# A two-layer block on one core: three places where the written order of TensorE's work is changed

## The chip, the core and the metric

The kernel runs on one core of a Trainium2 chip. A core has five engines with a queue each: TensorE (PE in the profile; its weight loads are listed as PEld), VectorE (DVE), ScalarE (ACT), GpSimd (POOL) and SyncE (SP), which here issues most of the DMA transfers. The metric is the device time of one execution in microseconds (us).

## The reference

Everything is float32. `x` and `ctx_1024` are 8 sequences (B) of 256 tokens (S) of 256 features (D), 2048 tokens (T) in all. Four residual steps follow each other:

```python
x = x + L0_xattn(layernorm(x), ctx, ctx)   # 1
x = x + L0_ffn(layernorm(x))               # 2
x = x + L1_xattn(layernorm(x), ctx)        # 3
x = x + L1_ffn(layernorm(x))               # 4
```

1. Sequences are projected to 16 features (`Wq`) after they are regrouped as 4 of 512 rows. The cyclic correlation of query and key over the features, averaged over everything else, gives a few weights and shifts. The value is rolled by each shift, summed with the weights, repeated for 16 heads and multiplied with `Wout`.
2. Eight experts with exactly 256 tokens each. Expert 0 takes the 256 tokens with the highest score against its centroid, expert 1 the best 256 of those left, and so on:

```python
for e in range(E):
    s = where(taken, -inf, scores[:, e]); _, idx = top_k(s, C); taken[idx] = True
h = gelu(einsum('ecd,edf->ecf', layernorm(routed), w1) + b1)   # F = 1024
out = routed + einsum('ecf,efd->ecd', h, w2) + b2              # back in token order
```

3. Cross attention with 16 heads of 16 features. Each sequence attends to the 256 rows of its own context, then comes an output product with `Wp`.
4. A mixture of experts: a router (softmax, top 2 of 8 experts), experts with `silu(x w1) * (x w3)` and `w2` of 1024 hidden features, and a shared expert of the same size; half of each is added.

## The kernel before, in words

The work is in one function, `fast_path`; `general_path` is there for data that do not fit the fast one's assumptions; every line that the trace names lies in the fast one. The tokens lie in SBUF as 16 tiles of 128 tokens on the partitions (P = 128), two tiles to a sequence (TPB = 2), in the tensor X. From line 1271 on the order is written by hand: each engine executes its instructions in the order in which the source calls them, and no scheduler moves them. If an instruction must wait for another engine, everything behind it on its own engine's queue waits too. Four stages follow each other in the trace.

**Front, 0 to 62 us.** Transposes of x and the context, scores' raw products and the correlation. Its last part is touched by the change. `copy_rows` (L1851) multiplies the two tiles of a sequence with the identity into a PSUM bank (`po`), without closing the sum; five of these are issued in a row, for the sequences `order_b[0]` to `order_b[4]`. Then come the "small products": `pb` (L1886, 8x8, which spreads the bound of each expert's scores over the partitions) and three pairs into `pw` (L1889, 32 columns each), which lie in one bank (tag "pg" of the pool `ps_a`, which has a single buffer). VectorE copies them out (`WCn`, `bound`). The same buffer is then used for `pr3` (L1924, four products of 128 columns: value times rolled weights), which VectorE scales to `R3` (L1932), and for `pp` (L1935, two products of 256 columns with `Wout`), to which VectorE adds the bias, giving `PB` (L1937). `spread_rows` (L1862, seen at L1867) adds `PB`'s rows to the open sums `po`, so that a bank then holds x after step 1. `take` (L1975) computes the statistics of a bank on VectorE, ScalarE copies it back to X, and its bank is free for the copy of a further sequence. 512 columns of these copies are one record in the trace where the matrix is 128x512.

**Search and expert products of step 2, 62 to 222 us.** For each expert, `search` (L2176) finds the 256th highest score in five rounds (ROUNDS). In a round VectorE counts the tokens above 32 thresholds (`count`), TensorE adds the counts up over the partitions (`pcn`), VectorE narrows the interval (`few`, `k`, `t`) and counts again. `list_tokens` (L2233) turns the chosen tokens into a list of indices in steps: VectorE marks them (`sel`, `taken`, L2245 to L2248), TensorE sums (`pse`, L2253), VectorE scans, TensorE places (`ppl`), VectorE makes two one-hot tensors (`oab`, `ob`, L2288 to L2291), TensorE joins them (`pid`, L2295) and spreads the result (`pix`), and GpSimd gathers the tokens' rows from DRAM (`R`) by an indirect DMA. While expert e is searched, the steps of the list of expert e - 1 are called one per round by `steps_of` (L2458), and `start_ffn` then queues the products of a finished list.

TensorE's idle time in these rounds is filled: `work` is a queue of pieces with a stated cost, and `fill(us)` (L1181) issues pieces until the stated costs reach the argument:

```python
while work and us > 0.3:
    cost, do = work.popleft(); do(); us -= cost
```

One product of an expert (`ph` of L2395 or `py` of L2412, 128x256) is stated at 0.43 us. A round is in the source `fill(each if r else head)`, the `pcn` product, `few`, `t`, the new count, and `next(steps)` at its end. The arguments of `head` and `each` come from FILLS (L2469) for experts 0 to 3 and are 2.58 and 2.58 for the others. The pieces thus stand ahead of `pcn`, and nothing stands between `pcn` and the list's product that `next(steps)` issues. SyncE's queue carries the loads of weights (`load_l0`, L1830), of `wp`, `bvc` and `bpb` before expert 5, and the writes of a blank row to the DRAM table Td (in `ffn`, L2349), which the last stage uses.

**Attention, 222 to about 363 us.** A unit is a sequence b and a half c of its heads. `queries` (L2635) multiplies the transposed normalised tokens `hT` with `wq` into a bank, from which ScalarE writes one half of QM and VectorE the other (L2654). `scores` (L2666) makes four products of 512 columns into `p`, ScalarE takes the exponentials; `values` (L2683) multiplies them with VA (value rows, made by `vals`). Ahead of it, step 2's output is added to X by `add_y` (L2572), which also has SyncE load the y of two sequences later; `batch_stats` (L2577) computes mean and variance on VectorE, a power on GpSimd, and a Newton step on GpSimd or VectorE; `norm_q` (L2611) writes the normalised tokens `h2` with one engine for each of the two tiles (seen at L2602); `turn_q` (L2631) transposes them on TensorE (L2626) and copies them to `hT` on VectorE. `add_bias` (L2615) adds `bpb` to X on GpSimd; `bpb` itself is the bias plus `pbp`, a product that holds one bank of `ps_m` until VectorE has read it. The loop at L2977 issues for each unit the first half of its scores, the values of the unit before, the second half and so on, with these steps between them. In the first units: `turn_q(1)`, `add_y(2)` and `batch_stats(2)` lie in unit (0,0), `norm_q(2)` in the middle of (0,1) with one tile on VectorE and one on GpSimd, `queries(1)` in the last part of (0,0) and `turn_q(2)` at the end of (0,1). `router_weights` (L2794: six small VectorE steps and two transposes of the router's matrix, each copied out by VectorE) is issued at the end of unit (2,0); what needs it is `route`, first called in unit (4,0).

**Step 4, 363 to 891.8 us.** The products of the shared expert and the eight experts; the change touches nothing in it.

Of the kernel before, what the change touches and what calls it, by code (L numbers as in the profile page):

```python
# [9 lines left out]
F32 = mybir.dt.float32  # L10
# [1076 lines left out]
def fast_path(  # L1087
# [785 lines left out]
                skip_group_check=True,  # L1873
            )

    for b in order_b[:4]:
        copy_rows(b, ps_t, "pt")
    copy_rows(order_b[4], ps_k, "pm")
    bnd = pa.tile([E, 1], F32, name="bnd")
    nc.vector.tensor_scalar(bnd, cs[:, 1:2], 1.01, None, ALU.mult)  # L1880
    bdiag = pa.tile([E, E], F32, name="bdiag")
# [1 line left out]
    WCn = pa.tile([P, 3, 32], F32, name="WCn")  # L1883
    pw = ps_a.tile([P, 4, 32], F32, tag="pg", name="pw")
    pb = pw[:, 3, 0:E]
    nc.tensor.matmul(pb, ones[:E, :], bdiag, start=True, stop=True)  # L1886
    for j in range(3):
        for dc in range(KC):
            nc.tensor.matmul(  # L1889
                pw[:, j, :],  # L1890
                wrt[:, dc, j * P : (j + 1) * P] if j < 2 else bt[:, dc, :],
                cenP[:, dc, :],
                start=(dc == 0),
                stop=(dc == KC - 1),
            )
    nc.vector.tensor_copy(WCn, pw[:, 0:3, :])
    bound = pr.tile([P, E], F32, name="bound")
    nc.vector.tensor_copy(bound, pb)
# [19 lines left out]
        allow_small_or_imprecise_dtypes=True,  # L1918
    )

    pr3 = ps_a.tile([P, 2, P], F32, tag="pg", name="pr3")
    for j in range(2):
        for sc in range(2):
            nc.tensor.matmul(  # L1924
                pr3[:, j, :],
                CW[:, sc, j * P : (j + 1) * P],
                vT[:, sc, :],
                start=(sc == 0),
                stop=(sc == 1),
            )  # L1930
    R3 = pa.tile([P, 2, P], F32, name="R3")
    nc.vector.tensor_scalar(R3, pr3, rtot, None, ALU.mult)  # L1932
    pp = ps_a.tile([P, D], F32, tag="pg", name="pp")
    for j in range(2):
        nc.tensor.matmul(pp, R3[:, j, :], woutr[:, j, :], start=(j == 0), stop=(j == 1))  # L1935
    PB = pa.tile([P, D], F32, name="PB")
    nc.vector.tensor_tensor(PB, pp, boutb, ALU.add)  # L1937

# [237 lines left out]
    def search(e, row, steps, head, each):  # L2176
# [25 lines left out]
        if e >= 2:  # L2202
            next(listers[e - 1])
        for r in range(ROUNDS):
            fill(each if r else head)
            pcn = ps_r.tile([P, 32], F32, tag="pcn", name="pcn")
            nc.tensor.matmul(
                pcn, cnt.to_broadcast([P, P]), B32h, start=True, stop=True
            )
            few = pm.tile([P, 32], F32, tag="few", name="few")  # L2210
            k = pm.tile([P, 1], F32, tag="k", name="k")
            nc.vector.tensor_scalar(
                few, pcn, CAP * (e + 1) + 0.5, None, ALU.is_lt, ALU.add, accum_out=k
            )
            if r < ROUNDS - 1:
                t = pm.tile([P, 1], F32, tag="t", name="t")
                nc.vector.scalar_tensor_tensor(
                    t, k, step[:, r, e : e + 1], w, ALU.mult, ALU.add
                )
                cnt = count(t)  # L2220
            nlo = pm.tile([P, 1], F32, tag="lo", name="lo", bufs=4)
            nc.vector.scalar_tensor_tensor(
                nlo, k, step[:, r, e : e + 1], lo, ALU.mult, ALU.add
            )
            lo = nlo
            if r < ROUNDS - 2:
                w = next_low(lo, r + 1)
            if r < ROUNDS - 1:
                next(steps)
        low.append((n, lo))  # L2230
        listers[e] = list_tokens(e, hand_over)
# [234 lines left out]
                start_ffn()  # L2466
            yield

    FILLS = ((0.43, 1.29), (2.15, 1.29), (2.15, 1.73), (2.15, 1.73))  # L2469
    for e in range(E - 1):  # L2470
        if e == 5:

# [8 lines left out]
                    )  # L2481
            nc.sync.dma_start(out=bpb, in_=L1_xattn_bp.partition_broadcast(P))
        search(
            e, rows.get(e), steps_of(e), *(FILLS[e] if e < len(FILLS) else (2.58, 2.58))
        )
        if e == 0:
            for k, _ in enumerate(listers[0]):
# [473 lines left out]
    for i in range(0, 4, 2):  # L2961
        list(vals(i, 2, ps_m))
    norm_q(0, nc.vector, nc.vector)
    nc.vector.tensor_tensor(bpb, bpb, pbp, ALU.add)
    hTs[0] = pq2.tile([P, KC, S], F32, tag="hT", name="hT")
    transpose_tokens(h2s[0], hTs[0], ps_m, "pm", 0)
    add_y(1)
    batch_stats(1, "q", nc.vector)
    queries(0, 0)
    queries(0, 1)  # L2970
    norm_q(1, nc.vector, nc.vector)
    add_bias(0)
    add_bias(1)
# [5 lines left out]
    for b in range(B):  # L2979
        for c in range(NB):  # L2980
            scores(b, c, 0)
            if prev:
                values(*prev, 0)
            send()
# [1 line left out]
                next(gates, None)  # L2986
            if prev is None:
                list(vals(4, 1, ps_m, nc.vector.tensor_copy))
                turn_q(1)
                add_y(2)  # L2990
                batch_stats(2, "q")
            elif c == 0:
                if b >= 2:
                    project_out(b - 2)
            else:
                if b >= 1:
                    turn_back(b - 1)
                if b >= 2:
                    turn_m(b - 2)
                if b + 2 < B:  # L3000
                    norm_q(b + 2, nc.vector, nc.gpsimd)
                    add_bias(b + 2)
            scores(b, c, 1)
            if gates:
# [8 lines left out]
            if gates:  # L3013
                next(gates, None)
            if c == 0:
                if b + 1 < B:
                    queries(b + 1, 0)
                    queries(b + 1, 1)
                if b + 2 < B and b:
# [5 lines left out]
            else:  # L3025
                if b >= 1:
                    turn_out(b - 1)
                if b + 2 < B:
                    turn_q(b + 2)
            if prev is None:  # L3030
# [27 lines left out]
                WS = load_l1(wsp, -1)  # L3058
            if (b, c) == (1, 0):
                router_columns()  # L3060
            if (b, c) == (2, 0):
                router_weights()
            prev = b, c


# [404 lines left out]
```

## Time and profile before

Three runs took 892.38, 890.15 and 886.46 us, with a median of 890.15 us. The profiled execution took 893.59 us by the same measure; its span, from the first to the last record, is 891.8 us, at a mean granted TensorE clock of 0.989 of full speed. The busy times by stage, in us (windows of the trace):

| stage | length | PE | DVE | ACT | POOL | clock | DMA share |
|---|---|---|---|---|---|---|---|
| front, 0-62 | 62 | 56.03 | 35.47 | 21.27 | 26.16 | 0.89 | 0.65 |
| search, 62-136 | 74 | 68.08 | 58.40 | 36.72 | 18.52 | 1.00 | 0.47 |
| search, 136-168 | 32 | 30.43 | 18.11 | 11.58 | 7.12 | 1.00 | 1.08 |
| rest of step 2, 168-222 | 54 | 52.75 | 12.57 | 17.44 | 11.46 | 1.00 | 0.38 |
| attention's start, 222-265 | 43 | 38.38 | 22.20 | 23.88 | 12.97 | 0.96 | 0.39 |
| attention, 265-363 | 98 | 95.41 | 61.20 | 67.03 | 51.01 | 1.00 | 0.05 |
| step 4, 363-891 | 528 | 523.04 | 101.28 | 87.36 | 86.41 | 1.00 | 0.38 |

How to read it: a busy row of the page gives the busy share in 40 slices of the span, 22.3 us each, in tenths; the row PEclk gives the clock that TensorE was granted, in tenths of full speed. In the timeline a line begins with the start in us, then the duration of the group, the engine, the source line, the operation with output and inputs, the shape and the number of instructions; in brackets stands how long the engine was idle before it and which instruction released it. "PE pid L2295 <- DVE ob L2291" in the list of waits means that TensorE's product pid stood for VectorE's ob. Ends of matmuls are modelled, so a busy TensorE may hold small holes.

### The profile page before, as it was taken

The numbers are of one execution on the slowest core, as the hardware profiler recorded it, in microseconds if no ns is written. First come the engines' busy times: TensorE is split into PE (matmuls) and PEld (weight loads), VectorE is DVE, ScalarE is ACT, GpSimd is POOL, SyncE is SP. The second block draws the span as 40 slices with busy tenths as digits, with TensorE's granted clock in tenths as the row PEclk, the third lists the DMA queues.
The fourth block names the chain that finished last, engine by engine and source line by source line (L and its number), as shares of the span: only waits on it lengthen the run. The fifth ranks groups of instructions, "written<-read, shape, count | busy, mean of one in ns | idle before, by whom it ended". The sixth has DMA issues, their size and how long they took to land.

```text
span 891.8 us, 11183 instructions
## 1 busy us (share of the span) xinstructions
PE 864.1 (97%) x4200; PEld 539.3 (60%) x4200; DVE 309.2 (35%) x1026; ACT 265.3 (30%) x495; POOL 213.6 (24%) x294
## 2 busy tenths in 40 slices
PE   9899899999899999999999999999999999999997
PEld 7546677878545555544748574646565656574745
DVE  7368876330635676453111111111111111111021
ACT  3244454242476767431010111111111111111110
POOL 7051221221324655233320011111101132111200
PEclk9879999999999999999999999999999999999999
DMA  7555259850250000081210636464656543311130
GB/s 246 180 175 182 83 174 319 249 189 31 57 151 13 14 7 32 19 324 50 73 55 24 189 107 177 148 182 149 162 170 147 182 92 107 89 12 12 18 101 28
DMA packets 86282, 105.21 MB, mean 118 GB/s; under 512 B 7979, under 2 KB 76812, under 8 KB 86188
## 3 DMA queue, kind: packets, MB, share of 16 engines
q1 hardware_dynamic: 77706, 91.10, 32.0%
q0 software_dynamic: 7920, 13.02, 7.0%
q8 instruction: 35, 0.57, 0.3%
q10 hardware_dynamic: 594, 0.30, 0.1%
q14 instruction: 27, 0.22, 0.1%
HBM read 80.60 MB, written 25.37 MB: 119 GB/s over the span
## 4 chain that ended last, share of the span: by engine, by line
PE 85%; DMA 5%; DVE 5%; POOL 1%; SPq 1%; issue 1%; ACT 1%; ACTq 0%; DVEq 0%; POOLq 0%
PE pgt L3090 19%; PE py L3112 19%; PE pu L3090 18%; PE ph L2395 4%; PE py L2412 4%; PE p L2673 4%; PE pv L2688 3%; DMA Td<-blank 2%; PE pp L2739 2%; PE pp L2640 2%; PE pp L1427 1%; PE po L1853 1%; DMA row<-SCd 1%; PE pgu L3285 1%; PE pt L3146 1%
## 5 line engine op out<-in xcount | busy, mean ns | idle before, releaser
L3099 DVE TENSOR_TENSOR A<-A,pu 128x512 f32<-128x512 f32 x96 | 66.1, 688 | 365.0 <-PE pu L3090 358.4
L3098 ACT ACTIVATE A<-pgt 128x512 f32<-128x512 f32 x96 | 57.4, 598 | 270.9 <-PE pgt L3090 270.8
L3159 POOL DMA_INDIRECT Od<-Y,ids x32 | 49.5, 1546 | 306.7 <-ACT Y L3172 211.6
L3090 PE MATMUL pgt<-RT,wa 128*128 128x512 f32 x256 | 121.1, 595 | 0.0
L3090 PE MATMUL pu<-RT,wb 128*128 128x512 f32 x256 | 120.3, 592 | 0.0
L3112 PE MATMUL py<-wc,A 128*128 128x256 f32 x512 | 111.8, 379 | 0.0
L3112 PEld LDWEIGHTS py<-wc,A 128*128 128x128 f32 x512 | 96.7, 190 | 13.3 <-issue 0.5
L2681 ACT ACTIVATE ex<-p,scale 128x512 f32<-128x512 f32 x128 | 77.2, 691 | 34.1 <-PE p L2673 34.1
L3090 PEld LDWEIGHTS pu<-RT,wb 128*128 128x128 f32 x256 | 48.6, 190 | 61.2 <-issue 60.0
L3090 PEld LDWEIGHTS pgt<-RT,wa 128*128 128x128 f32 x256 | 47.6, 190 | 54.9 <-issue 54.5
L2395 PE MATMUL ph<-RT,w 128*128 128x256 f32 x256 | 61.6, 387 | 2.1 <-ACT A L2404 2.1
L2412 PE MATMUL py<-w,A 128*128 128x256 f32 x256 | 59.7, 385 | 0.0
L2395 PEld LDWEIGHTS ph<-RT,w 128*128 128x128 f32 x256 | 45.4, 189 | 10.3 <-ACT A L2404 4.0
L2412 PEld LDWEIGHTS py<-w,A 128*128 128x128 f32 x256 | 47.3, 190 | 6.5
L2404 ACT ACTIVATE A<-ph,b1c 128x256 f32<-128x256 f32 x64 | 30.0, 473 | 69.0 <-PE ph L2395 67.3
L2673 PE MATMUL p<-QM,KT 32*128 32x512 f32 x256 | 45.2, 655 | 2.9 <-DVE QM L2654 2.9
L2913 POOL DMA_INDIRECT Td<-HP,to x32 | 31.6, 987 | 62.2 <-DMA Td<-HP,to 59.3
L3090 PE MATMUL pgt<-HT,wa_-1_2777 128*128 128x512 f32 x96 | 45.5, 596 | 0.0
L3090 PE MATMUL pu<-HT,wb_-1_2778 128*128 128x512 f32 x96 | 45.1, 592 | 0.0
L3172 ACT ACTIVATE Y<-py,R 128x256 f32<-128x256 f32 x32 | 15.2, 474 | 97.0 <-PE py L3112 93.5
L3112 PE MATMUL py<-wc_-1_2779,A 128*128 128x256 f32 x192 | 41.9, 379 | 0.0
L3112 PEld LDWEIGHTS py<-wc_-1_2779,A 128*128 128x128 f32 x192 | 36.4, 190 | 5.8 <-issue 1.0
(463 smaller groups left out, 1001.8 us busy)
## 6 DMA issues: line engine op xcount, KB each, us to landing
w<-in_L_ffn_w_dram SPq DMA_DIRECT2D x16, 1024.0 KB
wa<-in_L_ffn_w_e_dram SPq DMA_DIRECT2D x8, 1024.0 KB
wb<-in_L_ffn_w_e_dram SPq DMA_DIRECT2D x8, 1024.0 KB
wc<-in_L_ffn_w_e_dram SPq DMA_DIRECT2D x8, 1024.0 KB
R<-Td SPq DMA_DIRECT2D x8, 530.0 KB
sa<-in_L_ffn_w_e_dram SPq DMA_DIRECT2D x16, 256.0 KB
sb<-in_L_ffn_w_e_dram SPq DMA_DIRECT2D x16, 256.0 KB
sc<-in_L_ffn_w_e_dram SPq DMA_DIRECT2D x16, 256.0 KB
```

The costliest lines, as they stand in the source:

```text
L2395: nc.tensor.matmul(ph, w1[:, kc, f * P : (f + 1) * P], RT[:, kc, :], start=(kc == 0), stop=(kc == KC - 1),)
L2404: nc.scalar.activation(A[:, f, :], ph, AF.Gelu_apprx_tanh, bias=b1c[:, e, f : f + 1])
L2412: nc.tensor.matmul(py, A[:, f, r * P : (r + 1) * P], w2[:, f, :], start=(f == 0), stop=(f == NF - 1),)
L2673: nc.tensor.matmul(ps[g].rearrange("p m q -> p (m q)"), KT[rows, c, k0 : k0 + P], QM[b][rows, c].rearrange("p m q -> p (m q)"), start=True ...
L2681: nc.scalar.activation(e4[:, g], ps[g], AF.Exp, scale=scale)
L2688: nc.tensor.matmul(pvs[b, c][32 * g : 32 * g + 32, m, :], VA[:, b * TPB + kt, 8 * c + 2 * g + m, :], ex[b, c, kt][:, g, m, :], start=(kt = ...
L2913: nc.gpsimd.indirect_dma_start(out=Td, out_offset=bass.IndirectOffsetOnAxis(ap=to[g][:, k, j : j + 1], axis=0), in_=HP[:, GT * g + j, :], ...
L3090: nc.tensor.matmul(ps, w_[:, kc, fs], xs[kc], start=(kc == 0), stop=(kc == KC - 1),)
L3098: nc.scalar.activation(a, pgt, AF.Silu)
L3099: nc.vector.tensor_tensor(a, a, pu, ALU.mult)
L3112: nc.tensor.matmul(py, A[:, f, s : s + P], wc[:, f, :], start=(f == 0), stop=(f == NF - 1))
L3159: nc.gpsimd.indirect_dma_start(out=Od, out_offset=bass.IndirectOffsetOnAxis(ap=ids, axis=0), in_=Y, in_offset=None, compute_op=ALU.add,)
```

## The change

It edits three places.

*Front.* The copies of `order_b[3]` and `order_b[4]` are issued after the first and the second pair of small products, not before all of them, and `pb` is issued last. A helper `stay_warm` issues a product of the 128x128 matrix of ones with 256 columns of G, of which nothing reads the result: one after the `pr3` group and one after the `pp` group, into the second half of buffers that are made twice as large.

*Search.* From round 1 on 0.86 us less is filled ahead of `pcn`, and 0.86 us is filled after the new count, ahead of the list's step. The amount is now given for each round; that of round 2 of experts 2 and 3 is 2.58 where it was 1.73.

*Attention.* The addition of `pbp` to `bpb` follows the transposes of sequence 0. `queries(0)` comes ahead of `add_y(1)` and `batch_stats(1)`. `turn_q(1)`, `queries(1)`, `add_y(2)` and `batch_stats(2)` move to the middle of unit (0,1). `norm_q(2)`, with both tiles on VectorE, and `add_bias(2)` move to the end of (0,1), directly ahead of `turn_q(2)`. `norm_q(3)`, in unit (1,1), has both tiles on VectorE. `router_weights` moves from the end of unit (2,0) to behind the first half of the scores of unit (3,0).

```diff
-    for b in order_b[:4]:
+    for b in order_b[:3]:
         copy_rows(b, ps_t, "pt")
-    copy_rows(order_b[4], ps_k, "pm")
...
     pb = pw[:, 3, 0:E]
-    nc.tensor.matmul(pb, ones[:E, :], bdiag, start=True, stop=True)
     for j in range(3):
...
+        if j == 0:
+            copy_rows(order_b[3], ps_t, "pt")
+        elif j == 1:
+            copy_rows(order_b[4], ps_k, "pm")
+    nc.tensor.matmul(pb, ones[:E, :], bdiag, start=True, stop=True)
...
-    pr3 = ps_a.tile([P, 2, P], F32, tag="pg", name="pr3")
+    pr3 = ps_a.tile([P, 4, P], F32, tag="pg", name="pr3")
+
+    def stay_warm(ps, n):
+        for _ in range(n):
+            nc.tensor.matmul(ps, ones, G[:, 0, :], start=True, stop=True)
...
+    stay_warm(pr3[:, 2:4, :].rearrange("p a q -> p (a q)"), 1)
     R3 = pa.tile([P, 2, P], F32, name="R3")
-    nc.vector.tensor_scalar(R3, pr3, rtot, None, ALU.mult)
-    pp = ps_a.tile([P, D], F32, tag="pg", name="pp")
+    nc.vector.tensor_scalar(R3, pr3[:, 0:2, :], rtot, None, ALU.mult)
+    pp2 = ps_a.tile([P, 2, D], F32, tag="pg", name="pp")
+    pp = pp2[:, 0, :]
     for j in range(2):
         nc.tensor.matmul(pp, R3[:, j, :], woutr[:, j, :], start=(j == 0), stop=(j == 1))
+    stay_warm(pp2[:, 1, :], 1)
...
         for r in range(ROUNDS):
-            fill(each if r else head)
+            fill(each[r - 1] - 0.86 if r else head)
...
             if r < ROUNDS - 1:
+                fill(0.86)
                 next(steps)
...
-    FILLS = ((0.43, 1.29), (2.15, 1.29), (2.15, 1.73), (2.15, 1.73))
+    FILLS = {0: (0.43, [1.29] * 4), 1: (2.15, [1.29] * 4)}
+    FILLS[2] = FILLS[3] = (2.15, [1.73, 2.58, 1.73, 1.73])
...
-            e, rows.get(e), steps_of(e), *(FILLS[e] if e < len(FILLS) else (2.58, 2.58))
+            e, rows.get(e), steps_of(e), *FILLS.get(e, (2.58, [2.58] * 4))
...
     norm_q(0, nc.vector, nc.vector)
-    nc.vector.tensor_tensor(bpb, bpb, pbp, ALU.add)
     hTs[0] = pq2.tile([P, KC, S], F32, tag="hT", name="hT")
     transpose_tokens(h2s[0], hTs[0], ps_m, "pm", 0)
+    nc.vector.tensor_tensor(bpb, bpb, pbp, ALU.add)
+    queries(0, 0)
+    queries(0, 1)
     add_y(1)
     batch_stats(1, "q", nc.vector)
-    queries(0, 0)
-    queries(0, 1)
...
             scores(b, c, 0)
+            if (b, c) == (3, 0):
+                router_weights()
...
                 list(vals(4, 1, ps_m, nc.vector.tensor_copy))
+            elif b == 0:
                 turn_q(1)
+                queries(1, 0)
+                queries(1, 1)
                 add_y(2)
                 batch_stats(2, "q")
...
-                if b + 2 < B:
-                    norm_q(b + 2, nc.vector, nc.gpsimd)
+                if 2 < b + 2 < B:
+                    norm_q(b + 2, nc.vector, nc.vector if b < 2 else nc.gpsimd)
                     add_bias(b + 2)
...
-                if b + 1 < B:
+                if 0 < b and b + 1 < B:
                     queries(b + 1, 0)
...
                 if b >= 1:
                     turn_out(b - 1)
+                else:
+                    norm_q(2, nc.vector, nc.vector)
+                    add_bias(2)
                 if b + 2 < B:
                     turn_q(b + 2)
...
-            if (b, c) == (2, 0):
-                router_weights()
```

## The prediction

> **What bounds the kernel now.** I read the page's busy rows first. TensorE is busy in 97% of the span and carries 85% of the chain that ended last, so time can only come from its clock or from holes in its queue. The clock row shows two dips.
>
> ```profile
> PE   9899899999899999999999999999999999999997
> PEclk9879999999999999999999999999999999999999
> ```
>
> Windows of half a microsecond (columns: PE, PEld, DVE, ACT, POOL busy, then clock, DMA share, GB/s) date the dips.
>
> ```profile
> 40.00:40.50 0.50, 0.50 (x4) 0.50 (x4) 0.34 (x2) 0.00 (x0) 0.00 (x0) 0.52 0.93 334
> ...
> 53.50:54.00 0.50, 0.50 (x2) 0.00 (x0) 0.08 (x1) 0.50 (x2) 0.24 (x2) 0.83 0.17 63
> ```
> ```profile
> 234.50:235.00 0.50, 0.29 (x4) 0.29 (x8) 0.50 (x2) 0.00 (x0) 0.00 (x0) 0.58 0.00 0
> ...
> 237.50:238.00 0.50, 0.50 (x3) 0.41 (x2) 0.00 (x0) 0.50 (x3) 0.00 (x0) 0.51 0.00 0
> ```
>
> A mean of 0.52 is half clock from 40.02 on; 0.83 is half clock up to 53.67. That is 13.65 us. Likewise 234.58 to 237.99: 3.41 us, a quarter of it. The timeline shows what stood there.
>
> ```profile
> 37.12 0.38 PE L1886 MATMUL pw<-bdiag,ones 8*128 8x8 f32 x2
> ...
> 37.44 1.08 PE L1889 MATMUL pw<-cenP,wrt 128*128 128x32 f32 x8
> ...
> 39.43 1.51 PE L1924 MATMUL pr<-vT,CW 128*128 128x128 f32 x8 [0.47 <-PE pw L1889]
> ...
> 40.98 0.48 DVE L1932 TENSOR_SCALAR R<-pr,rtot 128x256 f32<-128x256 f32 x1 [0.60 <-PE pr L1924]
> ...
> 41.52 2.08 PE L1935 MATMUL pp<-woutr,R 128*128 128x256 f32 x4 [0.58 <-DVE R L1932]
> ...
> 44.11 2.09 PE L1867 MATMUL po<-PB,spread 32*128 32x512 f32 x8 [0.52 <-DVE PB L1937]
> ```
>
> The small products fill 37.12 to 38.96 but stream few columns. The waits of TensorE over the whole span name the other holes (total us, times, longest).
>
> ```profile
> PE pid L2295 <- DVE ob L2291: 3.3, 5, 1.2
> PE p L2673 <- DVE QM L2654: 2.9, 1, 2.9
> PE pse L2253 <- DVE sel L2248: 2.2, 4, 0.8
> ...
> PE pt L2626 <- POOL h L2602: 1.6, 2, 1.3
> ```
>
> [...] the QM writes needed at 231.53 (ACT's half done) ran at 234.12, behind the statistics of the next sequence.
>
> [...] Ten records of 512 columns took 4.56 us, about 0.43 each, [...]
>
> **Part 1, front.** (a) Interleaving moves seven small products; nothing is added. Each lies where it delays pr3 as before, so price 0 (bounds -0.3 to +0.2: weight loads may hide under a copy, or the identity is loaded again). [...] last copy now at about 37.1 to 37.95, then small ones and DVE's two reads, pr at 39.3. [...]
> (b) Two dense products, 128x256: two records each, 0.215 by L1427 (16 in 3.62), so 0.43. They are issued behind pr3 and pp, but the built program signals each group once, from its last product, the dense one: DVE's R3 and PB wait for them. So they lie on the path: +0.86, 1.7 at half clock. Bounds 0 (hidden after all) and 1.7. Queued behind: the spreads, then all statistics.
> (c) If the clock holds: pr 0.95 (five of its records ran in the first 0.59) + dense 0.43 + tail 0.2, R 0.48, pp 0.86 + dense 0.43 + tail 0.2, PB 0.42, hand-overs 0.15: 4.1 against 44.11 - 39.43 = 4.68. Gain 0.58. Then the first spread to the statistics of the last two copies: 11.27 before (44.11 to 55.38). At full clock VectorE leads: spread 1.1; six statistics at 0.53 to 4.3; ACT's copies free the banks at 4.45 and 4.95; two copies of x at 0.86 from 4.5 to 6.2; spread 1.1: 7.3. Gain 3.97. Front: -4.55. What is late next is VectorE's statistics.
>
> **Part 2, lists amid pieces.** 0.86 us of dense pieces moves from before the counting product to between it and the list's product; totals stay, except 0.86 more in one round each of experts 2 and 3, taken from work that runs later anyway. TensorE's waits for ob, oab and sel go: 3.3 + 0.4 + 2.2 = 5.9. VectorE is 8.3 to 8.9 of 10 us busy in 80 to 110; with round 2 of 2.58 it finishes ob (from place, 1.5 us) before the product wants it, so no count arrives late. From 136 to 168 DMA is saturated (share about 1): a gather of R issued at 139.16 and 140.45 was awaited by ACT to 149.60, and ACT also waited 0.94 for the Td fill. These move only with the SyncE queue, which issues from 118.78 to 134.65 without a break. I take off 0.7 for such waits (bounds 0 and 4). Net -5.2, bounds -7.7 (by starts rather than modelled ends: 89.57 to 90.94 is 1.3, not 1.2) and -1.5.
>
> **Part 3, attention's start.** The order of bpb lets QM go early, but it gives its bank later: the second transposes wait for the VA copy ending 229.45, not for 228.95, so ACT's QM moves from 230.97 to 231.27, ends 231.83; DVE 0.54; scores start 232.5, not 234.71. From there, at full clock:
> scores 1.14, so exponentials (2.42 a set) run 233.66 to 236.08 and to 238.52; the third set's last product needs that release, 238.6 + 1.1 = 239.7; values 239.63; turn_q(1) 240.63; its copy starts 0.74 later and takes 0.69: 242.06. Now queries(1) stands directly behind it, a bare wait of 0.8, and runs from 242.12. Second scores 244.04, values to 246.2. ACT's second QM ends 244.71, DVE's 245.3. Only then does VectorE add y(2) and take its statistics, 2.1 (239.55 to 241.64): 247.41. POOL's power and Newton steps 1.93: 249.34. Two h on DVE 0.72: 250.1. TensorE stands at turn_q(2), with scores(1,0,0) queued behind it: 250.6 against 249.41, +1.2. Bare from 246.2 to 250.1, 3.9 us, [...] half clock follows once more, 1.4 (3.41 x 0.83 busy / 2). The 249.41 held such a price already, so +2.6 by clock-free steps, of which 1.4 stands in for the old dip.
> Later: h(3) both on DVE takes away 1.32 of waiting. Router weights leave a place where TensorE lost 0.5 + 0.7 + 2 x 0.22 = 1.6; at the new one the two transposes cost 0.44 and perhaps 0.2: -1.0. SyncE's loads of y keep their order. Sum +0.3, bounds -2.3 (no dip, statistics earlier) and +2.5.
>
> **Sum.** -4.55 - 5.2 + 0.3 = -9.45 from the profiled execution's 893.59 (span 891.8): 884.1. That run is above the three runs shown (median 890.15). Taking off its dips, 4.55 + 0.86 + 1.4, gives 886.8, near the lowest, 886.46: I read their spread as dips caught or missed. Against the median the change is -0.7%.
>
> **Rivals.**
> R1, everything goes: search -7.7, and VectorE reaches y(2) early enough [...] (-1.4): 893.59 - 4.55 - 7.7 + 0.3 - 1.4 = 880.2. For it: waits by starts are longer than listed. Against: the strict queue behind QM(1).
> R2, the front still falls to half clock. [...] Then no 4.55, and the dense products cost up to 1.7: 893.59 + 0.9 - 5.2 + 0.3 = 889.6.
> R3, DMA holds the search: gathers and the Td fill end when they did, and TensorE waits for R instead: search -1.5, 887.8. For it: the chain of waits passes 16.42 us through Td. Against: those waits were 0.7 and 0.94 in all.
> R4, slower: the empty 3.9 us at turn_q(2) halves the clock, [...]; the front needed four windows. Each costs 1.4; one is in the forecast, so it passes 890.15 from 4.3 more windows, and with seven more it ends at 893.9. Against: the old dip at 234.58 ended after one window.
>
> **Numbers.** Forecast 0.53, R1 0.22, R2 0.12, R3 0.10, R4 0.03. Range 880.0 to 889.5: R1's point to R2's, leaving some 0.2 outside. One per cent (8.9 us) is about what a measurement can tell from no change. Faster by more (under 881.2): R1 0.20 and 0.06 of the forecast's own spread. Slower by more: 0.01 of R4's far end.
>
> **What would show it.** Front: clock 1.00 through 40 to 53, spreads starting near 43.5, the last statistics near 51; wrong if the clock row still dips. R3 starting 0.43 later than pr's end shows the dense product on the path. Search: waits of pid and pse near 0; a wait of prt or ACT's R for a DMA shows R3. Attention: first scores 2.2 after the queries less than before, then TensorE waiting some 3.5 us on h of L2602's counterpart, with half clock after it; wrong if that wait is under 1 us. [...]

## The result, and the profile after

The changed kernel takes 882.5 us in the median of ten runs (878.96 to 884.72), the kernel before, with its further runs, 887.55 us in ten (884.72 to 892.38): a ratio of 0.9937, 95% interval 0.9912 to 0.9961. The forecast was 884.1 us, 0.7% below the median then known; the gain is 0.6%, and it is clear of noise.

The profiled execution of the changed kernel took 878.96 us, span 877.3, against 893.59 and 891.8. That is 14.6 us, three times what the medians show. The two rows of the page that showed the dips before:

```profile
PE   8899999999799999999999999999999999999997
PEclk9999999999999999999999999999999999999999
```

The dip of the front is gone from the clock row. The timeline of TensorE in the front (start, duration, line, what, count, wait):

```profile
35.88 0.53 PE L1887 MATMUL pw<-cenP,wrt 128*128 128x32 f32 x4
36.24 1.10 PE L1853 MATMUL po<-X,ident 128*128 128x512 f32 x2
37.18 0.53 PE L1887 MATMUL pw<-cenP,wrt 128*128 128x32 f32 x4
37.54 1.11 PE L1853 MATMUL po<-X,ident 128*128 128x512 f32 x2
...
39.80 1.13 PE L1933 MATMUL pr<-vT,CW 128*128 128x128 f32 x8 [0.47 <-PE pw L1898]
40.76 0.60 PE L1929 MATMUL pr<-G,ones 128*128 128x256 f32 x2
41.94 1.13 PE L1946 MATMUL pp<-woutr,R 128*128 128x256 f32 x4 [0.58 <-DVE R L1942]
42.91 0.59 PE L1929 MATMUL pp<-G,ones 128*128 128x256 f32 x2
44.02 1.14 PE L1867 MATMUL po<-PB,spread 32*128 32x512 f32 x8 [0.52 <-DVE PB L1949]
```

The last copy now ends at 38.65 and not at 37.19. Each dense product lies on the path: R follows the end of the dense record (41.36) with VectorE's start at 41.40, not the end of pr, and PB likewise:

```profile
41.40 0.48 DVE L1942 TENSOR_SCALAR R<-pr,rtot 128x256 f32<-128x256 f32 x1 [0.66 <-PE pr L1929]
43.54 0.42 DVE L1949 TENSOR_TENSOR PB<-pp,boutb 128x256 f32<-128x256 f32 x1 [1.66 <-PE pp L1929]
```

TensorE's waits over the whole span (total us, times, longest):

```profile
PE pt L2640 <- DVE h L2616: 3.6, 1, 3.6
...
PE prt L2391 <- ACT R L2371: 0.4, 1, 0.4
...
PE pid L2308 <- DVE ob L2304: 0.2, 1, 0.2
```

The waits for ob and sel have gone, and the forecast's new wait for h is there, 3.6 us long. Windows of half a microsecond show the half clock that follows it (last three columns: clock, DMA share, GB/s):

```profile
239.00:239.50 0.50, 0.50 (x8) 0.01 (x2) 0.50 (x1) 0.00 (x0) 0.50 (x1) 1.00 0.56 174
239.50:240.00 0.50, 0.50 (x8) 0.20 (x8) 0.00 (x0) 0.13 (x1) 0.02 (x1) 0.69 0.06 20
...
243.00:243.50 0.50, 0.50 (x5) 0.00 (x0) 0.00 (x0) 0.00 (x0) 0.00 (x0) 0.90 0.00 0
```

By stages, from starts in the two timelines:

| from, to | before | after | difference | forecast |
|---|---|---|---|---|
| span's start to first pcn | 62.47 | 57.81 | -4.66 | -4.55 |
| first pcn to pbp (start of attention) | 161.87 | 154.97 | -6.90 | -5.2 |
| pbp to first pgt (start of step 4) | 139.02 | 137.04 | -1.98 | +0.3 |
| first pgt to the end | 528.44 | 527.48 | -0.96 | 0 |

Step 4 lasted 527.4 to 528.4 us in all traces, in no relation to the edits, so its 0.96 is chance. That the medians differ by only 5 us has to be explained by how typical the two profiles are.

**How the runs are read.** Each run comes with its mean granted clock. Within a kernel the times lie close to a line: fitted over 300 runs, those of the experiments and the ten of the changed kernel, with one slope for all, a run is 665 us times the missing clock above its kernel's time at full clock, with a scatter of 0.9 us. A stretch of 3.41 us at half clock lowers the mean by 0.0019, so by the fit it costs 1.3 us. Below, "at full clock" is a kernel's mean time less that term, uncertain by 0.1 to 0.5 us, and "clock loss" the term. The fit prices every such stretch alike; where the traces show one that cost less, the text says so, since the time at full clock then comes out too low. For the kernel before, the four sets of runs give 884.9 to 885.8 us at full clock and 3.7 to 5.8 us of loss. 75 of its 131 runs were at 0.993 or lower, which takes at least three or four such stretches; one of the 20 runs of the changed kernel was. Its ten runs above come to 878.8 us at full clock and its ten of experiment 5 to 880.2; this difference stays unexplained.

The starts and ends of half clock in one trace lie whole multiples of 3.413 us apart: in before, 234.58 is 57 of them after 40.02; in experiment 2, 50.68 and 67.74 are 3 and 8 after 40.44; in experiment 4, 60.46 and 251.61 are 6 and 62 after 39.98. Below, a window is one step of this grid. The grid kept its place over stretches at full clock (53.67 to 234.58 in before), so it is also used to say where a window ended while the clock held; that anything ends there is an assumption, which no trace shows.

### The profile page after: what moved, and what is told of

It reads as the page before. It is cut to its first block, busy times and chain, and to the rows that moved or that the text cites. A ratio compares the mean times of both kernels' runs of the same rounds, so it can differ in the third digit from the quotient of the medians.

```text
span 877.3 us, 11190 instructions
## 1 busy us (share of the span) xinstructions
PE 857.4 (98%) x4204; PEld 535.2 (61%) x4204; DVE 309.2 (35%) x1028; ACT 265.6 (30%) x495; POOL 211.1 (24%) x292
## 5 line engine op out<-in xcount | busy, mean ns | idle before, releaser
L2687 PE MATMUL p<-QM,KT 32*128 32x512 f32 x256 | 42.9, 650 | 0.4 <-DVE QM L2668 0.4
```

The source lines that it names most:

```text
L2687: nc.tensor.matmul(ps[g].rearrange("p m q -> p (m q)"), KT[rows, c, k0 : k0 + P], QM[b][rows, c].rearrange("p m q -> p (m q)"), start=True ...
```

## The experiments

**1. Interleaving alone**

```diff
-    for b in order_b[:4]:
+    for b in order_b[:3]:
...
+        if j == 0:
+            copy_rows(order_b[3], ps_t, "pt")
+        elif j == 1:
+            copy_rows(order_b[4], ps_k, "pm")
+    nc.tensor.matmul(pb, ones[:E, :], bdiag, start=True, stop=True)
```

> Only the interleaving of the copies and of the small products (pb last) is in, nothing else of the change. Theory 1 ([...]): no half clock in 36 to 54 us, the first pcn, at 62.5 us in the profile of before, comes at about 57.0 (4.55 for the clock and the hand-overs, 0.86 more because no dense product is on the path), attention and search as before. Against the kernel before: about 5 us less where that kernel had its dip, nothing where it had not, so 1 to 5 us in the median. Theory 2 (the two dense products hold the clock): half clock from about 40 us again, first pcn at 62 to 63, time as before within 1 us.

888.43 us against 890.88 (ratio 0.9977, interval 0.9957 to 0.9996). In its trace the clock is 1.00 from 36 to 56 us, as theory 1 expects (the copies between the small products hold it), and the first pcn starts at 56.19. The trace alone does not show that the edit held the clock: by the grid a window ended 2.30 us after pr's start in it, and with one ending at 2.11 us the clock was 1.00 with the old order as well (experiment 3). The runs do speak for the edit. At full clock it is 885.7, as before (885.8): the edit moves no work off the path. Its clock loss is 3.3 us against 5.4, and 6 of 22 runs were at 0.993 or lower against 45 of 75.

**2. Dense products alone**

```diff
+    stay_warm(pr3[:, 2:4, :].rearrange("p a q -> p (a q)"), 1)
...
+    stay_warm(pp2[:, 1, :], 1)
```

with the helper and the larger buffers.

> Only the two dense products behind pr3 and pp are in; the five copies stand together ahead of the small products as before. Theory 1 (the quiet stretch lies ahead of pr, where no dense product is): half clock from about 40 us as in before, and the two products lie on the path: first pcn at 63.3 to 64.2 us, time 0.9 to 1.7 us above before. Theory 2 (the dense products hold the clock): no half clock in 36 to 54 us, first pcn at about 58 us, time up to 4 us below before.

889.17 us (0.9981, 0.9958 to 1.0003). The trace goes with theory 1: half clock from 40.4 us, first pcn at 63.63.

```profile
39.50:40.00 0.50, 0.16 (x2) 0.05 (x1) 0.30 (x2) 0.00 (x0) 0.00 (x0) 1.00 1.00 385
40.00:40.50 0.50, 0.37 (x3) 0.40 (x4) 0.47 (x7) 0.00 (x0) 0.00 (x0) 0.94 1.06 393
40.50:41.00 0.50, 0.50 (x4) 0.50 (x4) 0.43 (x4) 0.00 (x0) 0.00 (x0) 0.50 0.91 356
```

A clock of 0.94 in the second line means that half clock began at about 40.44, 0.31 us after pr's start at 40.13. In the trace of before it was 0.59 us after, in that of experiment 4 0.43 us. All three dips begin just behind pr's start. In the runs it costs 0.45 us at full clock and loses less to the clock (4.5 against 5.4), so that the median is 1.7 us below before, where theory 1 had 0.9 to 1.7 above; 8 of 22 were at 0.993 or lower. By these counts the runs of experiments 1 and 2 (6 and 8 of 22) can't be told apart. In this trace the dense products, which come after the small ones, did not prevent the dip, but may have shortened it: it is back at full clock from 50.7 us, before at 53.67. It had another dip at 60.9.

**3. The search's part alone**

```diff
-            fill(each if r else head)
+            fill(each[r - 1] - 0.86 if r else head)
...
+                fill(0.86)
                 next(steps)
```

with the new amounts in FILLS.

> Only the pieces of 0.86 us between count and list step, and the new amounts, are in. Theory (TensorE's waits for ob, oab and sel go, no other wait takes their place): from the first pcn to the first py of the one-hot product, 160.15 us in the profile of before and 153.25 in that of the changed kernel, it is 152.5 to 154, waits of pid and pse under 0.3 us each; time 5.5 to 7.5 us below before. Rival (DMA holds the search, the waits return at R and Td): 157 to 159 us, time 1 to 3 below.

887.55 us (0.9962, 0.9940 to 0.9983). From the first pcn to the one-hot product it took 156.31 us, between the two expectations. The waits of TensorE over the whole span:

```profile
PE prt L2379 <- issue: 1.4, 1, 1.4
...
PE prt L2379 <- ACT R L2359: 0.7, 2, 0.5
...
PE pid L2296 <- DVE ob L2292: 0.2, 1, 0.2
```

The old waits went, as in the theory; a new one came, as in the rival: prt, the transposes of the gathered rows, for R of the seventh list. At full clock the gain is 3.9 us. This trace also holds the front of before with no dip in it (clock 1.00 from 36 to 56 us), first pcn at 56.85, 5.6 us earlier than in the profile of before. By the grid a window ended 2.11 us after pr's start in it; in the three traces with a dip one ended, and half clock began, 0.31 to 0.59 us after. The old front, then, ran both with the dip and without it. That the place of the windows decides is a reading of these four traces and was not tested by itself.

**4. Attention's part alone**

```diff
-    add_y(1)
-    batch_stats(1, "q", nc.vector)
     queries(0, 0)
     queries(0, 1)
+    add_y(1)
+    batch_stats(1, "q", nc.vector)
...
+            elif b == 0:
                 turn_q(1)
+                queries(1, 0)
+                queries(1, 1)
                 add_y(2)
                 batch_stats(2, "q")
```

with the rest of this part: bpb's addition, norm_q(2) and (3), the router's weights.

> Only attention's part is in: the order in the first units and the router's weights. Theory (steps as in the changed kernel): from the first py of the one-hot product to the first pgt, 140.74 us in the profile of before and 138.76 in that of the changed kernel, 138.5 to 139.2; TensorE waits 3.4 to 3.8 us for h of the third sequence; time 1.5 to 2.5 us below before. Rival (the empty 3.6 us halves the clock in most runs and that eats the gain of the other edits): 139.5 to 141, time within 1 us of before.

892.38 us (1.0010, 0.9990 to 1.0030), and 139.75 us from the one-hot product to pgt in the trace: the rival. TensorE waits 3.6 us for h and half clock follows, until 255.0 us. At full clock the part gains 1.2 us, but the clock loss is 7.2 us against 5.4. Part of that is the front's dip, which this trace has and which the edit does not touch, so the size of the price is better read from the next pair.

**5 and 6. The changed kernel again, and without attention's part.** The second keeps the front and the search's part and has attention as before.

> The changed kernel once more, beside its variants. Fitted over the runs of the first four experiments, a run's time is a time at full clock plus about 680 us times the missing clock: before 885.7, interleaving alone 885.6 to 886.1, dense products alone 885.9 to 886.1, search alone 881.8 to 882.0, attention alone 884.4. Theory (the parts add): 881.0 to 881.5 at full clock. Rival (the profile of the changed kernel is typical, in which TensorE waits 1.9 us less for the gather of the seventh list than with the search's part alone): 878.0 to 879.0. Half clock: front no more than one window of 3.41 us in nine runs of ten, attention one in most; mean clock 0.994 to 0.996.

> The changed kernel with attention's start and the router's weights as before. Theory (attention's part gives back 1.3 us at full clock and loses part of it to half clock): the time at full clock is 1.0 to 2.0 above that of the changed kernel, and the median within 0.5 to 2 us above. Rival (attention's part is worth nothing or costs, since its 3.6 us stall halves the clock): median at or below that of the changed kernel.

883.76 us (0.9934, 0.9906 to 0.9963) and 884.67 us (0.9938, 0.9913 to 0.9963), against 890.60 for before. At full clock 880.2 and 882.2 (experiment 5's theory had 881.0 to 881.5): by the fit attention's part gains 2.0 us, as experiment 6's theory had it, and its clock loss is 1.1 us higher (3.4 against 2.3). Net 0.9 us, within what the two intervals leave open; from the one-hot product to pgt the two traces take 139.75 and 140.69 us, 0.9 apart too. The parts add: 880.2 is 4.65 us below before's 884.85, and the parts measured alone give -0.1, +0.45, -3.9 and -1.2, which is -4.7. The profile first seen for the changed kernel was not typical. In the new one, from the first pcn to pbp, it took 158.8 us and not 155.0:

```profile
PE pt L2640 <- DVE h L2616: 3.6, 1, 3.6
PE prt L2391 <- ACT R L2371: 2.2, 2, 1.8
```

and windows show half clock behind this second wait too, from 175.71 to 179.12:

```profile
175.50:176.00 0.50, 0.50 (x3) 0.43 (x3) 0.00 (x0) 0.50 (x2) 0.00 (x0) 0.71 0.00 0
176.00:179.00 3.00, 3.00 (x9) 2.37 (x8) 0.00 (x0) 1.14 (x3) 0.00 (x0) 0.50 0.00 0
179.00:179.50 0.50, 0.50 (x4) 0.43 (x3) 0.00 (x0) 0.46 (x1) 0.00 (x0) 0.88 0.00 0
```

**7. y(2) ahead of turn_q(1)**

```diff
                 list(vals(4, 1, ps_m, nc.vector.tensor_copy))
+                add_y(2)
+                batch_stats(2, "q")
             elif b == 0:
                 turn_q(1)
                 queries(1, 0)
                 queries(1, 1)
-                add_y(2)
-                batch_stats(2, "q")
```

> The changed kernel, but y(2) is added and its statistics are taken in unit (0,0), behind vals(4), no longer behind the QM writes of queries(1). Theory (h of the third sequence is late because VectorE's queue is strict): the 3.6 us wait of pt for h falls under 1 us, no half clock near 240 us; time 2 to 4 us below the changed kernel. Rival (the exponentials on ScalarE set the pace there, the wait only stands where they would hold the next scores): the wait goes, but scores wait instead for p's banks, and the time is within 1 us of the changed kernel.

881.08 us (0.9903, 0.9866 to 0.9940), 2.7 below the changed kernel. Both expectations hold in part. The wait for h fell to 1.2 us, not under 1; that of the queries for hT rose from 0.8 to 1.8, since the copy of hT now stands behind y(2). By the fit nothing is gained at full clock (880.2 both times) and the whole gain is the clock, 1.05 us lost against 3.4. The traces divide it otherwise. From the one-hot product to pgt it takes 137.09 us, 2.66 less than in experiment 5. Of this, 1.31 is order: the two waits are 3.0 us together and no longer 4.4, and the first scores of sequence 1 come 16.50 us after the first of all, where the profile after has 17.81, both ahead of any half clock. The other half is the clock, and there the fit asks too much: the two windows of experiment 5 cost about 1.35 us, not twice 1.3. One hole of 3.6 us was followed by half clock, two of 1.8 and 1.2 were not.

**8. The changed kernel without dense products**

```diff
-    stay_warm(pr3[:, 2:4, :].rearrange("p a q -> p (a q)"), 1)
...
-    stay_warm(pp2[:, 1, :], 1)
```

> The changed kernel without its two dense products (the interleaving stays). Theory (the dense products lie on the path and only help to keep the clock): first pcn 0.9 us earlier where the clock holds, time at full clock 0.5 to 1.0 below the changed kernel; but [...] about one run in ten has the long half clock in the front again, 4.5 us: median 0.3 to 0.9 below. Rival (they are hidden by the hand-over to VectorE): first pcn the same within 0.2 us, median the same or above.

883.47 us (0.9911, 0.9890 to 0.9933), 0.3 below the changed kernel. From pr to the first pcn it takes 17.14 us instead of 18.01, so the two products cost 0.87 us of path, as forecast (0.86). In the runs they can't be told from nothing: 880.1 against 880.2 at full clock, clock loss 3.5 against 3.4; one run of 15 had a mean clock of 0.990 or less. The 0.87 us is seen in the traces only, and whether the products pay stays open.

**9. The blank rows of Td written later**

```diff
-    TPART = {2: (0, 12), 3: (12, 24), 4: (24, E * CAP1 // P + 1)}
+    TPART = {6: (0, 19), 7: (19, E * CAP1 // P + 1)}
```

> The changed kernel, but the blank rows of Td (three transfers of 1.6 to 1.7 MB, in the changed kernel issued at 111, 127 and 142 us) are written in two transfers with experts 6 and 7 instead of three with 2, 3 and 4. In the traces of six kernels that have the search's part, prt of the seventh list waits 0.4 to 2.4 us for the gather of R, and in two of them a half clock window follows. Theory (transfers saturate 130 to 160 us, so GpSimd's write of Yd is late and the gathers queued behind it too): DMA share in 140 to 160 us falls under 0.9, the wait for R falls under 0.5 us, first pcn to pbp 154.5 to 156 us; median 1 to 2.5 us below the changed kernel. Rival (the gather meets the load of the eighth expert's weights at 167.9 us, whatever came before): the wait stays at 1.4 to 2.4 us, time within 0.7 us.

Experiments 9 to 12 ran beside other runs of before (median 888.30, for 12 891.42; 890.60 for 5 to 8), so their distance to the changed kernel is taken from the times at full clock, each against its own before; the changed kernel is 4.65 us below.

880.05 us (0.9898, 0.9871 to 0.9925). At full clock it is 7.6 us below before, so the edit gains 2.9. From the first pcn to pbp it took 154.40 us, and prt waited for R nowhere. Windows of ten microseconds of the run of experiment 5, and then of this one (last two columns DMA share and GB/s):

```profile
130.00:140.00 10.00, 10.00 (x55) 8.25 (x54) 8.19 (x38) 2.84 (x7) 3.22 (x3) 1.00 1.11 291
140.00:150.00 10.00, 10.00 (x69) 8.16 (x67) 5.30 (x25) 3.13 (x8) 3.06 (x3) 1.00 1.07 350
150.00:160.00 10.00, 9.59 (x69) 7.74 (x65) 4.10 (x20) 5.62 (x12) 1.97 (x2) 1.00 1.08 313
```
```profile
130.00:140.00 10.00, 10.00 (x55) 8.23 (x54) 8.19 (x37) 2.91 (x7) 3.22 (x3) 1.00 0.55 160
140.00:150.00 10.00, 10.00 (x68) 8.15 (x67) 5.28 (x25) 3.03 (x7) 4.07 (x4) 1.00 0.45 144
150.00:160.00 10.00, 10.00 (x70) 8.39 (x68) 4.11 (x20) 5.61 (x12) 0.99 (x1) 1.00 0.58 154
```

The transfers had filled the engines; now they are half full. GpSimd's timeline shows the link. Experiment 5, then this run:

```profile
158.50 0.98 POOL L2435 DMA_INDIRECT Yd<-Y,ids  x1 [6.25 <-DVE ob L2304]
165.65 0.97 POOL L2435 DMA_INDIRECT Yd<-Y,ids  x1 [6.17 <-issue]
166.93 0.99 POOL L2327 DMA_INDIRECT R<-NMd,ids  x1 [0.31 <-DVE ids L2324]
168.22 0.96 POOL L2327 DMA_INDIRECT R<-NMd,ids  x1 [0.30 <-DMA Yd<-Y,ids]
```
```profile
163.53 0.97 POOL L2435 DMA_INDIRECT Yd<-Y,ids  x1 [10.31 <-DVE m L2320]
164.80 0.99 POOL L2327 DMA_INDIRECT R<-NMd,ids  x1 [0.30 <-issue]
166.10 0.96 POOL L2327 DMA_INDIRECT R<-NMd,ids  x1 [0.30 <-DVE ids L2324]
```

VectorE had written Y at 163.99 and at 163.26. With the transfers full, GpSimd's write of Yd began 1.7 us later, with them half full 0.3 us later, and the four gathers of R stand behind it in GpSimd's queue.

The landings of the transfers show what it waited for. The write of Yd before it, issued at 158.50, landed 6.4 us later, at 164.92, and the next began 0.73 us after that. In all seven traces with the search's part and Td's old place this distance is 0.73 or 0.74 us. In this run the write before it, issued at 152.23, had landed at 156.24. The trace of before names the same wait at another pair of writes:

```profile
151.54 0.98 POOL L2422 DMA_INDIRECT Yd<-Y,ids  x1 [7.64 <-DMA Yd<-Y,ids]
```

So the writes of Yd went one after the other in these traces, and the one behind the stretch with a DMA share of 1.08 took 6.4 us to land, the one in a stretch with 0.58 only 4.0. Why 1.7 us of delay cost more than that at prt shows in SyncE's queue, which issues the load of the eighth expert's weights. In experiment 5 that load was issued at 167.68 and the seventh list's second gather at 168.22, behind it; ScalarE had R at 174.43, 6.2 us later. In this run the gather (166.10) came ahead of the load (166.94), and nothing waited. The split is the same everywhere: in the six traces in which prt waits 1.8 us or more the gather is issued after the load, by 0.1 to 1.2 us, in the four with 0.4 us or less (the profile after, experiments 9, 11 and 12) 0.4 to 0.8 us ahead of it. The rival thus named the right transfer, but whether the gather came behind it or ahead of it followed, in these ten traces, from what had come before. The order of these two was not changed by itself.

**10. y(2) between turn_q(1) and queries(1)**

```diff
                 turn_q(1)
+                add_y(2)
+                batch_stats(2, "q")
                 queries(1, 0)
                 queries(1, 1)
-                add_y(2)
-                batch_stats(2, "q")
```

> The changed kernel, but y(2) is added and its statistics are taken between turn_q(1) and queries(1), where VectorE was idle for 1.8 us in the trace of the changed kernel. Theory (the place in VectorE's strict queue alone sets when h is there): pt's wait for h falls from 3.6 to about 1.5 us, the wait of queries for hT stays 0.8, the first scores of sequence 1 come 2.0 to 2.3 us earlier after the first scores of all (17.8 us before), no half clock near 240 us; median 2.5 to 3.5 below the changed kernel. Rival (as with the earlier place, what is taken from one wait comes back in another): 16.3 us or more, median no lower than with the earlier place.

880.36 us (0.9909, 0.9880 to 0.9938). At full clock it is 6.1 us below before, 1.4 more than the changed kernel, and it loses 1.6 us to the clock instead of 3.4: together 3.2, the theory. As in experiment 7 the fit puts too much of it down to the clock. The wait for h is 1.2 us, that for hT 0.8, and the first scores of sequence 1 come 15.43 us after the first of all (17.81 before the edit, 16.50 in experiment 7), 2.4 us earlier.

**11 and 12. Together, and h ahead of ov.** Experiment 11 has the edits of 9 and 10. Experiment 12 also moves norm_q(2):

```diff
+            if (b, c) == (0, 1):
+                norm_q(2, nc.vector, nc.vector)
+                add_bias(2)
             if prev:
                 values(*prev, 1)
                 keep(*prev)
...
-                else:
-                    norm_q(2, nc.vector, nc.vector)
-                    add_bias(2)
                 if b + 2 < B:
                     turn_q(b + 2)
```

> Both edits, Td late and y(2) between turn_q(1) and queries(1). Theory (they act in separate stages and add): 3.5 to 5.5 us below the changed kernel in the median, 877.5 to 880.5 us. Rival (the fills of Td now delay the loads of y at the start of attention, first scores late): above the run with y(2) moved alone.

> Td late and y(2) between turn_q(1) and queries(1), and norm_q(2) with add_bias(2) ahead of the last values of unit (0,0) and of the copy ov, behind which h of the third sequence stood in VectorE's queue for 0.7 us. Theory (queue order): h waits only for GpSimd's Newton steps, pt's wait falls from 1.2 to 0.4 to 0.6 us, the first scores of sequence 1 come 14.6 to 15.0 us after the first scores of all (15.4 before), median 0.4 to 0.9 below that of the run with both edits, 876.3 to 876.8. Rival (the exponentials then set the pace and the scores wait for a bank instead): the next groups of scores end when they did, median within 0.3.

877.19 us (0.9861, 0.9833 to 0.9889) and 875.52 us (0.9829, 0.9797 to 0.9861; before 891.42 beside it). Both came out a little below what was expected. In the last trace the wait for h is short, and the scores then wait a little for the exponentials (1.52 us where eight take 1.14):

```profile
233.97 0.78 PE L2640 MATMUL pt<-ident,h 128*128 128x128 f32 x4 [0.37 <-DVE h L2616]
234.68 1.52 PE L2687 MATMUL p<-QM,KT 32*128 32x512 f32 x8
```

They start 14.58 us after the first scores. It is the fastest version found, 1.7% below the kernel before. At full clock the two are 9.3 and 10.1 us below before, and both lose 0.9 us to the clock.

## Why the prediction was right, and where it was not

**Sign and size** were right: 0.7% forecast, 0.6% measured, with an interval of 0.4 to 0.9%, finer than the one per cent that the prediction thought could be told. Against the repeated runs of experiment 5 the mean gain is 6.7 us: 4.65 at full clock and 2.1 less lost to the clock. The steps, in their order:

**Front (-4.55).** In the two profiles it is right to 0.1 us, and the step "dense products lie on the path, +0.86" is right too (0.87). But 4.55 was counted in full, from an execution that had the dip, although the prediction itself read the spread of the runs as dips caught or missed. 57% of before's runs had a clock of 0.993 or lower, and in the mean of the runs the front saves about 3 us of clock (clock loss 5.5 in before, 2.3 with front and search, where the search's part alone lost 5.6 against 5.4). From this the dense products take 0.87 back in the traces, 0.1 to 0.45 in the runs (experiments 8 and 2).

That the small products ahead of pr bring the dip, and that copies between them hold the clock, was the author's estimate. The traces, sorted by the end of a window (by the grid) behind pr's start, show when half clock came:

| traces | order of the front | window ends after pr's start | half clock there |
|---|---|---|---|
| before, experiments 2 and 4 | old | 0.59, 0.31, 0.43 us | yes |
| experiment 3 | old | 2.11 us | no |
| experiments 11, 6, 12, 10 | interleaved | 0.41, 0.74, 0.74, 0.98 us | no |
| after, experiments 1, 5, 7, 8, 9 | interleaved | 1.9 to 3.4 us | no |

The dense product starts 0.96 us after pr (40.76 and 39.80 in the profile after), so behind the end of the window in experiments 11, 6 and 12. If a dip there would have begun at that end, as the three seen did, the dense product came too late to stop it, and of the edits to the front only the interleaving stands ahead. The runs agree: of those with interleaving and the search's part, 2 of 81 were at 0.993 or lower, in experiment 8 without dense products 1 of 15, against 30 of 44 in experiments 3 and 4 with the old front. The new front is not free of half clock either: it began at 56.38 in experiment 7 and at 56.83 in experiment 11, for one window.

**Search (-5.2).** TensorE's waits for ob and sel went as forecast: up to the end of the search (first pcn to pcs) the trace of experiment 3 gains 5.0 us, 115.45 to 110.45. The term "0.7 for such waits" was too small: R is waited for 1.8 to 2.4 us in six of the seven traces that have this part and Td's old place, 0.4 in the other, which happened to be the profile after. So rival R3 named the right resource, but of the 3.7 us that it took off the forecast the runs show 1.3: the part gains 3.9 us at full clock, between the forecast's 5.2 and R3's 1.5. R3's "for" was the evidence that I set aside: the stretch with a DMA share of about 1, and a path through Td. It acts through the writes of Yd and the order of a gather and a load (experiment 9).

**Attention (+0.3).** Its timing was the most exact. First scores 9.88 us after the one-hot product were forecast, and 9.83 came; h waited for 3.9, and 3.6 came; one window at half clock followed. The step that failed is "half clock follows once more, 1.4". From scores(1,0,0) to the next queries it took 6.05 us in that window and 5.68 before at full clock, 0.4 more: scores there stood for the exponentials anyway, and a slower TensorE used up that wait. The prediction priced the window by TensorE's busy share alone. That 1.4 is near the price of a usual run is luck: three of the five traces with this wait had two windows, and in experiment 5 the two cost about 1.35. Router weights gave 1.6 instead of 1.0, h(3) 1.5 instead of 1.3. In the runs the part gains 1.2 to 2.0 us at full clock and pays 1.1 or more of it back by the fit. The traces give a gain of 1.3 at full clock: 139.75 us from the one-hot product to pgt in experiment 2, which had no half clock there, and 138.4 for the new order (9.84 and 17.81 up to scores(1,0,0), 110.75 from there in experiment 10). The forecast's +0.3 held the old dip in its starting point and was about 1 us too high.

**Why it ended near 884.** Errors cancelled: the front was overrated for a typical run by some 2 us and the search by 1.3, attention was underrated by about 1, and the profile the sum started from was 3.4 us above the median of its runs. R1 (everything goes) is what the profile after shows and not what the runs do. R2 did not come: no trace with the new front has half clock at pr. R4 did not come: the half clock after the wait lasted one or two windows, never seven.

## What to carry to other kernels

Compare the clock of every run, not only of the profiled one: a profile that caught a dip, or missed it, can make a change look three times its worth, and a fit of time against clock separates what work an edit moved from what it did to the clock. That fit prices all half clock alike, so check it on the traces: in experiment 5 two windows behind a wait cost about 1.35 us together, not 2.6. One trace in which the clock held proves little: of four with the old front one held it. A hole on the bounding engine costs its length, and more if half clock follows: at attention's start it did after the wait of 3.6 us in five traces of five, after that of 2.9 us in four of five, and not after two of 1.8 and 1.2; behind prt's longest wait in experiment 5, 1.8 us, it did. When an edit takes a wait away, look at which shared resource was full behind it; here it was the transfers, and moving transfers that nobody needed yet was worth nearly as much as the largest of the change's three parts.

## What the runs showed of the hardware

- Half clock followed a stretch of TensorE without a long hole in it: in the trace of before the longest wait between 36.6 and 40.0 us is 0.47 and TensorE was busy for 2.93 us of these 3.40, but from 37.12 to 38.96 with products of 8 and 32 columns; half clock began at 40.02. In the three traces of the old front with this dip it began 0.31 to 0.59 us after pr's start; in the fourth (experiment 3) the clock was 1.00 from 36 to 56 us.
- An indirect write of GpSimd (Yd) landed 2.4 us after its issue at 165.65 in experiment 5, and 6.4 us after its issue at 158.50, behind the stretch with a DMA share of 1.08.
- VectorE took longer while GpSimd added bpb. In experiment 7 the addition of y(2) took 1.65 us while GpSimd's ran, elsewhere 0.68:

```profile
230.10 1.27 POOL L2632 TENSOR_TENSOR X<-X,bpb 128x512 f32<-128x512 f32 x1 [1.47 <-DVE h L2616]
```
```profile
230.27 1.65 DVE L2588 TENSOR_TENSOR X<-X,yg 128x512 f32<-128x512 f32 x1
```

  VectorE's lasted nearly as long as its own time and what was left of GpSimd's together (0.68 + 1.10). In the same trace an instruction of VectorE on two columns (b_t<-b_r,b_ve) took 1.23 us beside another such addition; in the trace of before it took 1.22 beside one (232.39, GpSimd's from 232.33) and 0.16 with none beside it (227.1).
